# Attention by pairs of graphs, with scores as four row tiles of 32 rows, in a two-layer graph network on one core

## The chip, the cores and the metric

The kernel runs on one core of one Trainium2 chip. A core has five engines that run side by side, each in its own order: TensorE (matrix products), VectorE, ScalarE, GpSimd, and SyncE, which here only issues transfers (DMA). The metric is the device time of one run in microseconds (us). Before the change the median of three runs is 2892.74 us (2891.68 to 2894.03).

## The reference, cut to what matters

Input are 128 graphs of 128 nodes with 256 features each, all in 32-bit floats, and an integer adjacency matrix of 0 and 1 for each graph. Layer 0 has two graph attentions (GAT), a normalisation, a feed-forward of width 1024 and a second normalisation. Layer 1 is attention with 8 heads of 32 features, whose value weights depend on the relation that the adjacency names:

```
q = (src @ Wq + bq);  k = (src @ Wk + bk)              # 8 heads of 32
scores = einsum('bhid,bhjd->bhij', q, k) / sqrt(32)
attn = softmax(scores, axis=-1)
for r in range(4):
    v_r = src @ Wv[r] + bv[r]
    out += einsum('bhij,bhjd->bhid', attn * (adj == r), v_r)
x = layernorm(src + out @ Wo + bo)
x = layernorm(x + gelu(x @ W1 + b1) @ W2 + b2)
```

With an adjacency of 0 and 1 only two relations occur; the program tests this at its start and takes its "binary" arm. Only that arm runs here.

## The kernel before, in words

**Tiling and stages.** Four graphs form a group (G = 4), so there are 32 groups. Each group goes through five stages: load, gat, ff0 (the first feed-forward), att (the attention of layer 1) and ff1. A stage is a Python generator that emits a part of its work and then yields a number of planned time. The function `layers` keeps all stages of all groups in a heap, ordered by planned time: group g starts at PERIOD * g plus the stage's entry in `begin`, and each yield moves it on by an entry of `TIMES`. So stages of several groups are woven into each other. While the plan runs, every TensorE instruction from planned time 280 on, and every transfer from the start, is tied to the one emitted before it. TensorE and the DMA queue of SyncE therefore work in the order of emission, and an instruction that waits holds up all that stand behind it. The other engines get their order from a scheduler when the program is built, and also keep it at run time.

**The attention of a group.** `features` makes the transposed features T of the group's tokens. `transposed` has two ways. The direct one uses TensorE and the identity. The other, taken for all groups but those at the two ends, transposes blocks of 32 by 32 on VectorE (L288), stores the tile with four transfers to a scratch tensor in device memory (L291, `zd`) and loads it back in block order with one transfer (L293). That load must wait until the stores have landed. From T come the queries (L468) and the keys (L474). The keys are written twice by ScalarE (L476) into the tile `kbd`, with a 0/1 factor by row, so that each block of 64 rows holds a block-diagonal matrix of two heads.

`weights(b)` makes the softmax of one graph. Its scores (L490) are four matmuls: for each half i of the features, two row tiles of 64 rows, each with 128 query columns as weights and 256 moving columns of `kbd` (two heads). A 32-bit matmul is two records in the profile, so a graph has 8. Then VectorE takes maxima (L496), ScalarE the exponentials with their sums (L500), VectorE the reciprocals (L501), GpSimd the products (L502); each half of the heads has its own maximum, sum and product. `turned` transposes the weights (tile e to eT) through the same `transposed`. `by_relation` multiplies them with the mask (L515, tile m), `values` makes the values (L531, VectorE adds the bias at L532), `weighted` multiplies weights and values (L544: 16 matmuls of 32 columns by 128, four column tiles side by side, 32 records a graph), and ScalarE copies the result (L548). The product with `wo` (L577) is added to the tokens at L578.

These steps are emitted graph by graph: scores of graphs 0 and 1 first, then for each graph b its weighting, the scores of graph b + 2, the values of b + 1, `wo`, the transpose of b + 2 and the mask of b + 1.

**What runs around it.** `feed_forward` makes ff0 and ff1: products L333 on partial sums (GpSimd, L309 to L312), sums and functions on ScalarE and VectorE (L339 to L360), the second matrix at L378, the addition to the tokens at L388. `gat_block` has its products at L435, L443 and L454, and softmax at L410 to L424; it sends two small rows through device memory (L405, L407). `normalised` takes the statistics on VectorE (L256, L257), some small steps on GpSimd and the scaling on ScalarE (L265); `affine` (L271) is GpSimd's.

PSUM holds eight buffers: seven of the name `mm`, used in turn by all products, and one `av` for L544.

Of the kernel before, what the change touches and what calls it, by code (L numbers as in the profile page):

```python
# [24 lines left out]
P = 128  # L25
G = 4
Q = 32
# [2 lines left out]
TIMES = {  # L30
    "sums": 5, "ff visits": (2.5, 2.5, 3, 3, 3.25, 3.25, 3.25, 3.25), "ff2": 3,
    "ff first half": 10, "ff half": 5, "row": 16, "gat": 19, "wh": 5.5,
    "gat copy": 2, "qk": 4.5, "scores": 5.5, "turn0": 10, "turn1": 5,
    "v0": 5.5, "av": 9, "v": 4, "wo": 4, "turn": 3, "mask": 3,
    "lead ff0": 26, "lead att": 32, "lead ff1": 32, "affine": 7,
    "store": 25,
}
STAGES = "load", "gat", "ff0", "att", "ff1"

GENERAL = dict(  # L40
    binary=False, times=TIMES, period=430, bufs=dict(T=3, tok=2, m=4, mm=6, v=1),
    begin=dict(load=-87, gat=-51, ff0=48, att=132, ff1=300), early={},
    kept={PE: 0, SP: 0},
)

BINARY = dict(
    binary=True, times=TIMES,
    period=100, bufs=dict(T=5, tok=5, m=1, mm=7, v=2),
    begin=dict(load=-87, gat=-51, ff0=48, att=132, ff1=300),
    early={  # L50
        (1, "ff0"): 48,
# [34 lines left out]
def constants(tc, a, c, cst, tmp, ps):  # L86

    nc = tc.nc
    D, DC, R, MW = c.D, c.DC, c.R, c.MW
    T = G * P  # L90
# [55 lines left out]
    def others():  # L146

        ln_rows = cst.tile([P, len(KS), 2, D], F32, name="ln_rows")
        nc.sync.dma_start(ln_rows, on_all_rows(0, 8))
        plus = tmp.tile([P, 3, D], F32, name="plus")  # L150
        nc.sync.dma_start(plus, on_all_rows(8, 3))
        nc.vector.tensor_add(ln_rows[:, :3, 1], ln_rows[:, :3, 1], plus)
        c.ln = {k: (ln_rows[:, n, 0], ln_rows[:, n, 1]) for n, k in enumerate(KS)}
        c.wf2 = wload("wf2")
        c.wq = wload("wq")
        c.wk = wload("wk")
        c.wv = wload("wv")
        c.bv = cst.tile([P, R * D], F32, name="bv")
        nc.sync.dma_start(c.bv, on_all_rows(11, R))
        c.wo = wload("wo")  # L160
        c.w1 = wload("w1")
        c.w2 = wload("w2")
        c.kbd = [cst.tile([P, G, 2, P], F32, name=f"kbd{n}") for n in range(DC)]
        c.own = cst.tile([P, 2], F32, name="own")
        nc.vector.memset(c.own, 0.0)
        for q in range(P // Q):
            nc.vector.memset(c.own[ts(q, Q), q % 2:q % 2 + 1], 1.0)
        c.bk_own = [cst.tile([P, DC], F32, name=f"bk{q}") for q in range(2)]
        c.sums = {n: [cst.tile([P, w.shape[-1] // 2], F32, name=f"{n}s{i}") for i in (1, 2, 4)]
                  for n, w in (("wf1", c.wf1), ("w1", c.w1))}  # L170

# [44 lines left out]
def per_row(v, n):  # L216

    return v[:, :, None].to_broadcast([P, v.shape[-1], n])


def stages_of(tc, a, out, c, pools, plan):
# [73 lines left out]
    def t_tile():  # L295
        return wk.tile([P, G * MW], F32, name="T", bufs=TB)[:, :G * D]
# [162 lines left out]
    def attention(y, g, first, direct):  # L459
# [2 lines left out]
        at = load_mask(g)  # L462
        yield TIMES["lead att"]
        qT = t_tile().rearrange("p (c t) -> p c t", c=DC)
        for i in range(DC):
            p = ps.tile([P, T], F32, name="mm")
            for f in range(DC):
                nc.tensor.matmul(p, c.wq[:, f, ts(i, P)], hT[:, :, f], start=f == 0, stop=f == DC - 1)  # L468
            nc.vector.tensor_scalar(qT[:, i], p, c.col["bq"][:, i:i + 1], SCALE, op0=OP.add, op1=OP.mult)

        for i in range(DC):
            p = ps.tile([P, G, N], F32, name="mm")
            for f in range(DC):
                nc.tensor.matmul(p, c.wk[:, f, ts(i, P)], hT[:, :, f], start=f == 0, stop=f == DC - 1)  # L474
            for q in range(2):
                nc.scalar.activation(c.kbd[i][:, :, q], p, AF.Identity, scale=c.own[:, q:q + 1],  # L476
                                     bias=c.bk_own[q][:, i:i + 1])

        if not binary:
            adj = ps.tile([P, G, N], F32, name="adj", bufs=1)  # L480
            nc.vector.tensor_copy(adj, at)

        def weights(b):


            scores = [ps.tile([P, DC, 2, N], F32, name="mm") for _ in range(2)]
            for i in range(DC):
                for h in range(2):
                    rows = ts(h, P // 2)
                    nc.tensor.matmul(scores[h][:, i], qT[rows, i, ts(b, N)], c.kbd[i][rows, b],  # L490
                                     start=True, stop=True, tile_position=(h * P // 2, 0))
            e = wk.tile([P, H, N], F32, name="e1")
            for h, p in enumerate(scores):
                p = p.rearrange("p c q n -> p (c q) n")
                nm = sm.tile([P, HC], F32, name="nm1")
                nc.vector.tensor_reduce(nm, p, AX.X, OP.max, negate=True)  # L496
                s = sm.tile([P, HC], F32, name="s1")
                eh = e[:, ts(h, HC)]
                for q in range(HC):
                    nc.scalar.activation(eh[:, q], p[:, q], AF.Exp, bias=nm[:, q:q + 1], accum_out=s[:, q:q + 1])  # L500
                nc.vector.reciprocal(s, s)  # L501
                nc.gpsimd.tensor_mul(eh, eh, per_row(s, N))  # L502
            return e

        def turned(e):
            eT = wk.tile([P, H, N], F32, name="eT")
            transposed(e, eT, direct, e)
            return eT
# [27 lines left out]
        def weighted(ms, v):  # L536

            po = ps.tile([P, DC, N], F32, name="av", bufs=1)

            order = range(RV) if binary else range(RV - 1, -1, -1)  # L540
            for i in range(DC):
                for n, r in enumerate(order):
                    for q in reversed(range(HC)):
                        nc.tensor.matmul(po[ts(q, DH), i], v[:, r, i * P + q * DH:i * P + (q + 1) * DH],  # L544
                                         ms[r][:, q // 2 * HC + i * 2 + q % 2],
                                         start=n == 0, stop=n == RV - 1, tile_position=(0, q * DH))
            oT = wk.tile([P, DC, N], F32, name="oT")
            nc.scalar.copy(oT, po)  # L548
            return oT

        RV = 2 if binary else R
        yield TIMES["qk"]
        es = [weights(0)]
        yield TIMES["scores"]
        es.append(weights(1))
        yield TIMES["turn0"]
        eT = [turned(es[0])]
        yield TIMES["turn1"]
        eT.append(turned(es[1]))
        yield TIMES["v0"]  # L560
        PARTS = range(R)
        v, ms = values(0), by_relation(0, eT[0], range(R))
        for b in range(G):
            more = b + 1 < G
            affine(y, "02", b, 1)
            yield TIMES["av"]
            oT = weighted(ms, v)

            if b + 2 < G:
                es.append(weights(b + 2))  # L570
            yield TIMES["v"]
            if more:
                v = values(b + 1)
            yield TIMES["wo"]
            p = ps.tile([P, D], F32, name="mm")
            for i in range(DC):
                nc.tensor.matmul(p, oT[:, i], c.wo[:, i], start=i == 0, stop=i == DC - 1)  # L577
            nc.vector.tensor_add(y[:, b], y[:, b], p)  # L578
            yield TIMES["turn"]
            if b + 2 < G:  # L580
                eT.append(turned(es[b + 2]))
            yield TIMES["mask"]
            if more:
                ms = by_relation(b + 1, eT[b + 1], range(R))
        yield 1
        normalised(y)
        return y
# [11 lines left out]
def layers(ctx: ExitStack, tc: tile.TileContext, a: dict, out: bass.AP, c, plan: dict):  # L599
# [21 lines left out]
    def stage_attention(g):  # L621
        if g == 0:
            folded(nc, c, pools.ps, c.wq, c.col["bq"], "02")
            folded(nc, c, pools.ps, c.wk, c.col["bk"], "02")
            for q in range(2):
                nc.vector.tensor_scalar(c.bk_own[q], c.col["bk"], c.own[:, q:q + 1], None, op0=OP.mult)
# [156 lines left out]
```

## Time and profile before

| what | busy, us | share of 2890.0 us | instructions |
|---|---|---|---|
| TensorE matmuls | 2787.7 | 96% | 15554 |
| TensorE weight loads (beside the matmuls) | 2166.1 | 75% | 15554 |
| ScalarE | 1724.3 | 60% | 5191 |
| GpSimd | 1597.4 | 55% | 1866 |
| VectorE | 1504.7 | 52% | 3072 |
| DMA queue of SyncE, share of 16 engines | | 49.1% | 1156704 packets |

| row of the profile | count | busy, us |
|---|---|---|
| L490, scores, TensorE | 1024 records | 147.7 |
| L544, weighting, TensorE | 4096 records | 211.9 |
| L476, key tile, ScalarE | 128 | 92.6 |
| L500, exponentials, ScalarE | 1024 | 362.1 |
| L502, products, GpSimd | 256 | 269.4 |
| L515, mask, VectorE | 128 | 186.2 |
| idle time of L515 for the transfer eT<-zd | 92 waits | 374.8 |

A row's busy time is the time in which at least one of its instructions is under way; matmuls overlap, so the mean length of one is longer than the distance between two. The chain of waits goes back from the last instruction of the run, at each step to what released it: what stands there set the time. The idle time of an engine that isn't in the chain costs nothing.

### The profile page before, as it was taken

To read this page: it belongs to the slowest core of one execution; us is meant where nothing else is said; L and a number is where in the kernel's file an instruction comes from. 1 tells how busy PE (TensorE), PEld (TensorE's weight loads), DVE (VectorE), ACT (ScalarE), POOL (GpSimd) and SP (SyncE) were. 2 spreads that over 40 slices of the span, in tenths; PEclk is the share of its full clock that TensorE was granted. 3 is DMA by queue.
4 is the path that set the end of the run, shared out by engine and by line. 5 is a ranking of instruction groups with operands and counts; after the bars stand their busy time and mean duration, and the time that the engine had idled before them with its cause. 6 is when DMAs were issued, how large, how long until landed. Compare 5 with 4: busy or idle time off the path is not lost.

```text
span 2890.0 us, 45554 instructions
## 1 busy us (share of the span) xinstructions
PE 2787.7 (96%) x15554; PEld 2166.1 (75%) x15554; DVE 1504.7 (52%) x3072; ACT 1724.3 (60%) x5191; POOL 1597.4 (55%) x1866
## 2 busy tenths in 40 slices
PE   4996999999999999999999999999999999999988
PEld 3764777777877777777777787777778777777756
DVE  5444545545545555554554555555565545555442
ACT  3445566566666666666656666666666675666543
POOL 1434556556655556665655665565566565556553
PEclk7998999999999999999999999999999999999999
DMA  7145454555554556555445545454654544564310
GB/s 275 45 104 121 104 118 106 110 132 127 119 114 107 113 117 139 114 119 118 106 108 131 129 113 125 104 111 117 137 128 107 123 106 111 122 135 106 77 37 15
DMA packets 1156945, 328.69 MB, mean 114 GB/s; under 512 B 903008, under 2 KB 1126752, under 8 KB 1156064
## 3 DMA queue, kind: packets, MB, share of 16 engines
q1 hardware_dynamic: 1156704, 325.68, 49.1%
q8 instruction: 126, 2.06, 0.3%
q14 instruction: 115, 0.94, 0.1%
HBM read 195.97 MB, written 129.62 MB: 113 GB/s over the span
## 4 chain that ended last, share of the span: by engine, by line
PE 71%; DMA 7%; DVE 6%; POOL 5%; ACT 4%; issue 2%; SPq 2%; DVEq 0%; POOLq 0%; ACTq 0%
PE mm L378 25%; PE mm L333 19%; PE mm L531 5%; PE mm L474 4%; PE mm L468 4%; PE mm L490 4%; PE av L544 3%; PE mm L435 3%; PE mm L577 3%; POOL tok L271 2%; DMA zd<-e 2%; SPq L291 2%; DMA eT<-zd 2%; PE mm L454 1%; DMA zd<-T 1%
## 5 line engine op out<-in xcount | busy, mean ns | idle before, releaser
L271 POOL TENSOR_TENSOR tok<-tok,ln_rows 128x512 f32<-128x512 f32 (+1 forms) x596 | 669.5, 1133 | 34.4 <-PE mm L282 11.1
L500 ACT ACTIVATE e<-mm,nm 128x128 f32<-128x128 f32 x1024 | 362.1, 397 | 239.2 <-DVE nm L496 229.6
L378 PE MATMUL mm<-w,fT 128*128 128x256 f32 x2048 | 460.6, 381 | 0.0
L378 PE MATMUL mm<-wf,fT 128*128 128x256 f32 x2048 | 456.6, 381 | 1.5 <-ACT fT L354 1.5
L378 PEld LDWEIGHTS mm<-w,fT 128*128 128x128 f32 x2048 | 386.6, 190 | 74.2 <-issue 24.2
L502 POOL TENSOR_TENSOR e<-e,s 128x512 f32<-128x512 f32 x256 | 269.4, 1053 | 300.5 <-DVE s L501 299.8
L378 PEld LDWEIGHTS mm<-wf,fT 128*128 128x128 f32 x2048 | 386.5, 190 | 64.3 <-issue 9.2
L515 DVE TENSOR_TENSOR m<-eT,am 128x1024 f32<-128x1024 f32 x128 | 186.2, 1454 | 385.2 <-DMA eT<-zd 374.8
L496 DVE TENSOR_REDUCE nm<-mm 128x4 f32<-128x512 f32 x256 | 162.9, 676 | 254.6 <-PE mm L490 254.6
L265 ACT ACTIVATE tok<-tok,nmr,rstd 128x256 f32<-128x256 f32 x480 | 249.9, 603 | 20.1 <-POOL nmr L263 20.0
L531 PE MATMUL mm<-wv,T 128*128 128x512 f32 x512 | 249.3, 610 | 0.0
L352 POOL TENSOR_TENSOR fT<-fT 128x512 f32<-128x512 f32 x128 | 163.3, 1277 | 153.8 <-ACT fT L351 153.8
L500 ACT ACTIVATION_READ_ACCUMULATOR e<-mm,nm 128x1 f32 x1024 | 242.9, 237 | 0.0
L354 ACT ACTIVATE fT<-fT,col 128x512 f32<-128x512 f32 x256 | 170.4, 715 | 118.8 <-DVE fT L348 117.1
L309 POOL TENSOR_TENSOR t<-T 128x256 f32<-128x256 f32 x64 | 47.6, 744 | 321.3 <-DMA T<-zd 321.0
L333 PE MATMUL mm<-T,w 128*128 128x256 f32 x768 | 202.3, 386 | 4.0 <-DMA T<-zd 2.9
L424 POOL TENSOR_TENSOR e<-e,s 128x512 f32<-128x512 f32 (+1 forms) x68 | 68.1, 1002 | 244.4 <-DVE s L423 230.6
L333 PE MATMUL mm<-T,wf 128*128 128x256 f32 x768 | 193.1, 381 | 0.0
L256 DVE BATCH_NORM_STATS2 st<-tok 128x6 f32<-128x256 f32 x480 | 176.7, 409 | 2.4
L333 PEld LDWEIGHTS mm<-T,w 128*128 128x128 f32 x768 | 144.4, 192 | 30.6 <-issue 6.5
L422 ACT ACTIVATE e<-e,nm 128x128 f32<-128x128 f32 x256 | 101.6, 430 | 105.2 <-DVE nm L419 98.8
L333 PEld LDWEIGHTS mm<-T,wf 128*128 128x128 f32 x768 | 146.1, 191 | 21.7 <-issue 0.8
(144 smaller groups left out, 5147.1 us busy)
## 6 DMA issues: line engine op xcount, KB each, us to landing
zd<-e SPq DMA_DIRECT2D x496, 128.0 KB, 4.6
eT<-zd SPq DMA_DIRECT2D x124, 512.0 KB, 4.4
zd<-T SPq DMA_DIRECT2D x364, 128.0 KB, 3.5
T<-zd SPq DMA_DIRECT2D x91, 512.0 KB, 4.2
xt<-in_xT_dram SPq DMA_DIRECT2D x32, 512.0 KB, 5.0
e<-zsd SPq DMA_DIRECT2D x60, 256.0 KB, 3.3
tok<-in_x_dram SPq DMA_DIRECT2D x30, 512.0 KB
out_dram<-tok SPq DMA_DIRECT2D x29, 512.0 KB, 5.4
```

The source lines that it names most:

```text
L256: nc.vector.bn_stats(st, y[:, b])
L265: nc.scalar.activation(y[:, b], y[:, b], AF.Identity, bias=nmr[:, b:b + 1], scale=rstd[:, b:b + 1])
L271: engine.tensor_tensor(y[:, b:b + n], y[:, b:b + n], v[:, None, :].to_broadcast([P, n, D]), op)
L333: nc.tensor.matmul(p[:, i], win[k][:, ts(f0 + i, P)], hs[k], start=first and i == 0, stop=True, skip_group_check=True)
L352: nc.gpsimd.tensor_add(hi[:, :, 1], hi[:, :, 1], hi[:, :, 0])
L354: nc.scalar.activation(lo[:, i], lo[:, i], func, bias=bin_[:, f0 + i:f0 + i + 1])
L378: nc.tensor.matmul(ys[b // 2][:, b % 2], fT[f][:, ts(b, N)], wout[:, f], start=b % 2 == 0 and n == 0, stop=n == FC - 1, skip_group_check=True)
L496: nc.vector.tensor_reduce(nm, p, AX.X, OP.max, negate=True)
L500: nc.scalar.activation(eh[:, q], p[:, q], AF.Exp, bias=nm[:, q:q + 1], accum_out=s[:, q:q + 1])
L502: nc.gpsimd.tensor_mul(eh, eh, per_row(s, N))
L515: nc.vector.tensor_tensor(m, eT, at[:, b][:, None, :].to_broadcast([P, H, N]), OP.mult)
L531: nc.tensor.matmul(p, hT[:, b, f], wv[:, f, r:r + 2], start=f == 0, stop=f == DC - 1)
```

## The change

The attention works on two graphs at a time (`together=2`). The key tile is plain: `kT`, written once by ScalarE. The scores of a pair are 16 matmuls: for each graph and each half of the features, four row tiles of 32 rows (one head each), with 128 query columns as weights and 128 moving key columns. Each of the four row tiles has a PSUM buffer of its own, which holds both graphs and both halves. The purpose is to let four small matmuls run in the array at once and to drop the zeros that the block-diagonal tile carries through it. The softmax then has one maximum for each buffer, one reciprocal for the pair, and one product for each graph. Weights, transposes, masks, values, weighting, `wo` and its addition also go by pairs, so the steps between the yields change, and with them the planned times and the order of emission. Below, "i" is the half of the features and "q" the row tile.

```diff
-    "gat copy": 2, "qk": 4.5, "scores": 5.5, "turn0": 10, "turn1": 5,
-    "v0": 5.5, "av": 9, "v": 4, "wo": 4, "turn": 3, "mask": 3,
+    "gat copy": 2, "qk": 7, "scores": 11, "turn": 14, "mask": 11, "av": 10,
+    "wo": 8, "turned": 3,
...
-    period=100, bufs=dict(T=5, tok=5, m=1, mm=7, v=2),
+    period=100, bufs=dict(T=5, tok=5, m=2, mm=7, v=2),
...
+        kT = wk.tile([P, DC, T], F32, name="kT", bufs=1)
...
-            for q in range(2):
-                nc.scalar.activation(c.kbd[i][:, :, q], p, AF.Identity, scale=c.own[:, q:q + 1],
-                                     bias=c.bk_own[q][:, i:i + 1])
+            nc.scalar.activation(kT[:, i], p, AF.Identity, bias=c.col["bk"][:, i:i + 1])
...
-        def weights(b):
-            scores = [ps.tile([P, DC, 2, N], F32, name="mm") for _ in range(2)]
-            for i in range(DC):
-                for h in range(2):
-                    rows = ts(h, P // 2)
-                    nc.tensor.matmul(scores[h][:, i], qT[rows, i, ts(b, N)], c.kbd[i][rows, b],
-                                     start=True, stop=True, tile_position=(h * P // 2, 0))
-            e = wk.tile([P, H, N], F32, name="e1")
...
+        def weights(bs):
+            n = len(bs)
+            scores = [ps.tile([P, n, DC, N], F32, name="mm") for _ in range(HC)]
+            for j, b in enumerate(bs):
+                for i in range(DC):
+                    for q in range(HC):
+                        rows = ts(q, DH)
+                        nc.tensor.matmul(scores[q][:, j, i], qT[rows, i, ts(b, N)], kT[rows, i, ts(b, N)],
+                                         start=True, stop=True, tile_position=(q * DH, 0))
+            es = [wk.tile([P, DC, HC, N], F32, name="e1") for _ in bs]
+            s = sm.tile([P, HC, n, DC], F32, name="s1", bufs=2)
+            for q, p in enumerate(scores):
+                nm = sm.tile([P, n * DC], F32, name="nm1", bufs=8)
+                nc.vector.tensor_reduce(nm, p.rearrange("p j i n -> p (j i) n"), AX.X, OP.max, negate=True)
+                for j in range(n):
+                    for i in range(DC):
+                        k = j * DC + i
+                        nc.scalar.activation(es[j][:, i, q], p[:, j, i], AF.Exp, bias=nm[:, k:k + 1],
+                                             accum_out=s[:, q, j, i:i + 1])
+            r = sm.tile([P, n, DC, HC], F32, name="r1", bufs=2)
+            nc.vector.reciprocal(r.rearrange("p j i q -> p q j i"), s)
+            for j, e in enumerate(es):
+                es[j] = e.rearrange("p i q n -> p (i q) n")
+                nc.gpsimd.tensor_mul(es[j], es[j], per_row(r[:, j].rearrange("p i q -> p (i q)"), N))
+            return es
...
+        STEP = plan["together"]
         yield TIMES["qk"]
-        es = [weights(0)]
+        es = weights(range(STEP))
         yield TIMES["scores"]
-        es.append(weights(1))
-        yield TIMES["turn0"]
-        eT = [turned(es[0])]
-        yield TIMES["turn1"]
-        eT.append(turned(es[1]))
-        yield TIMES["v0"]
...
+        eT = [turned(e) for e in es]
+        for b in range(0, G, STEP):
+            bs = range(b, b + STEP)
+            yield TIMES["turn"]
+            vs = [values(k) for k in bs]
+            affine(y, "02", b, STEP)
+            yield TIMES["mask"]
+            parts = [(by_relation(k, e, range(R)), v) for k, e, v in zip(bs, eT, vs)]
             yield TIMES["av"]
-            oT = weighted(ms, v)
-
-            if b + 2 < G:
-                es.append(weights(b + 2))
-            yield TIMES["v"]
...
+            oT = weighted(parts)
+            if b + STEP < G:
+                es = weights(range(b + STEP, b + 2 * STEP))
             yield TIMES["wo"]
...
+            if b + STEP < G:
+                yield TIMES["turned"]
+                eT = [turned(e) for e in es]
```

`weighted` takes a pair of graphs with one `av` buffer and one copy, the `wo` products of a pair share a PSUM buffer and one addition, and the tiles `kbd`, `own` and `bk_own` and what fills them are gone. The other arm's plan gets `together=1` and other times; it doesn't run.

More of the change, by code (lines that the diff above doesn't have):

```diff
@@ L40 @@
 GENERAL = dict(
-    binary=False, times=TIMES, period=430, bufs=dict(T=3, tok=2, m=4, mm=6, v=1),
-    begin=dict(load=-87, gat=-51, ff0=48, att=132, ff1=300), early={},
+    binary=False, times=TIMES, together=1, period=560, bufs=dict(T=3, tok=2, m=4, mm=6, v=1),
+    begin=dict(load=-87, gat=-51, ff0=48, att=132, ff1=400), early={},
     kept={PE: 0, SP: 0},
@@ L46 @@
 BINARY = dict(
-    binary=True, times=TIMES,
-    period=100, bufs=dict(T=5, tok=5, m=1, mm=7, v=2),
+    binary=True, times=TIMES, together=2,
+    period=100, bufs=dict(T=5, tok=5, m=2, mm=7, v=2),
     begin=dict(load=-87, gat=-51, ff0=48, att=132, ff1=300),
@@ L162, in others @@
         c.w2 = wload("w2")
[L163 to L168, printed above, removed]
         c.sums = {n: [cst.tile([P, w.shape[-1] // 2], F32, name=f"{n}s{i}") for i in (1, 2, 4)]
@@ L471, in attention @@
         for i in range(DC):
-            p = ps.tile([P, G, N], F32, name="mm")
+            p = ps.tile([P, T], F32, name="mm")
             for f in range(DC):
                 nc.tensor.matmul(p, c.wk[:, f, ts(i, P)], hT[:, :, f], start=f == 0, stop=f == DC - 1)
-            for q in range(2):
-                nc.scalar.activation(c.kbd[i][:, :, q], p, AF.Identity, scale=c.own[:, q:q + 1],
-                                     bias=c.bk_own[q][:, i:i + 1])
+            nc.scalar.activation(kT[:, i], p, AF.Identity, bias=c.col["bk"][:, i:i + 1])
         if not binary:
@@ L481, in attention @@
             nc.vector.tensor_copy(adj, at)
-        def weights(b):
-            scores = [ps.tile([P, DC, 2, N], F32, name="mm") for _ in range(2)]
-            for i in range(DC):
-                for h in range(2):
-                    rows = ts(h, P // 2)
-                    nc.tensor.matmul(scores[h][:, i], qT[rows, i, ts(b, N)], c.kbd[i][rows, b],
-                                     start=True, stop=True, tile_position=(h * P // 2, 0))
-            e = wk.tile([P, H, N], F32, name="e1")
[L493 to L503, printed above, removed]
+        def weights(bs):
[23 more added lines that the diff above has]
+            return es
@@ L534, in values, with weighted @@
             return v
-        def weighted(ms, v):
-            po = ps.tile([P, DC, N], F32, name="av", bufs=1)
+        def weighted(parts):
+            n = len(parts)
+            po = ps.tile([P, n, DC, N], F32, name="av", bufs=1)
             order = range(RV) if binary else range(RV - 1, -1, -1)
[L541 to L547, printed above, removed]
+            for j, (ms, v) in enumerate(parts):
+                for i in range(DC):
+                    for k, r in enumerate(order):
+                        for q in reversed(range(HC)):
+                            nc.tensor.matmul(po[ts(q, DH), j, i], v[:, r, i * P + q * DH:i * P + (q + 1) * DH],
+                                             ms[r][:, i * HC + q],
+                                             start=k == 0, stop=k == RV - 1, tile_position=(0, q * DH))
+            oT = wk.tile([P, n, DC, N], F32, name="oT", bufs=1)
             nc.scalar.copy(oT, po)
@@ L551, in attention @@
         RV = 2 if binary else R
+        STEP = plan["together"]
         yield TIMES["qk"]
-        es = [weights(0)]
+        es = weights(range(STEP))
         yield TIMES["scores"]
-        es.append(weights(1))
-        yield TIMES["turn0"]
-        eT = [turned(es[0])]
-        yield TIMES["turn1"]
-        eT.append(turned(es[1]))
-        yield TIMES["v0"]
[L561 to L565, printed above, removed]
-            yield TIMES["av"]
-            oT = weighted(ms, v)
-            if b + 2 < G:
-                es.append(weights(b + 2))
-            yield TIMES["v"]
-            if more:
-                v = values(b + 1)
-            yield TIMES["wo"]
[L575 to L584, printed above, removed]
+        eT = [turned(e) for e in es]
[6 more added lines that the diff above has]
+            parts = [(by_relation(k, e, range(R)), v) for k, e, v in zip(bs, eT, vs)]
+            yield TIMES["av"]
+            oT = weighted(parts)
+            if b + STEP < G:
+                es = weights(range(b + STEP, b + 2 * STEP))
+            yield TIMES["wo"]
+            p = ps.tile([P, STEP, D], F32, name="mm")
+            for j in range(STEP):
+                for i in range(DC):
+                    nc.tensor.matmul(p[:, j], oT[:, j, i], c.wo[:, i], start=i == 0, stop=i == DC - 1)
+            nc.vector.tensor_add(y[:, b:b + STEP], y[:, b:b + STEP], p)
+            if b + STEP < G:
+                yield TIMES["turned"]
+                eT = [turned(e) for e in es]
         yield 1
@@ L624, in stage_attention @@
             folded(nc, c, pools.ps, c.wk, c.col["bk"], "02")
-            for q in range(2):
-                nc.vector.tensor_scalar(c.bk_own[q], c.col["bk"], c.own[:, q:q + 1], None, op0=OP.mult)
             folded(nc, c, pools.ps, c.wv, c.bv, "02", rows=True)
```

## The prediction

> **What bounds the kernel now.** I read the page's shares first, then the chain of waits over one group in mid run, then the DMA queue's timeline, then the few places where TensorE stood still. The page:
>
> ```profile
> PE 2787.7 (96%) x15554; PEld 2166.1 (75%) x15554; DVE 1504.7 (52%) x3072; ACT 1724.3 (60%) x5191; POOL 1597.4 (55%) x1866
> PE 71%; DMA 7%; DVE 6%; POOL 5%; ACT 4%; issue 2%; SPq 2%; DVEq 0%; POOLq 0%; ACTq 0%
> ```
>
> TensorE is near full, nothing else above 60%. The chain of waits from 1400 to 1500 us (start, length, what):
>
> ```profile
> 1410.69 1.06 PE mm L490 x8
> 1411.75 1.01 PE av L544 x32
> 1412.76 1.06 PE mm L490 x8
> 1413.83 3.65 PE mm L378 x16
> ...
> 1481.96 3.43 PE mm L468 x8
> 1485.40 3.43 PE mm L474 x8
> 1488.83 6.91 PE mm L378 x32
> 1495.74 1.06 PE mm L490 x8
> ```
>
> Every piece is TensorE's and each begins where the last ends: from the first scores of one group to those of the next, 85.05 us (85.2 over 27 groups) without a wait. So shorter TensorE work shows at once, and so does any new wait of TensorE. The transposes run beside it, on one DMA queue, and in order:
>
> ```profile
> 1424.64 2.56 SPq L291 DMA_DIRECT2D zd<-e  x4
> 1430.01 0.38 SPq L293 DMA_DIRECT2D eT<-zd  x1
> 1430.49 4.21 SPq L291 DMA_DIRECT2D zd<-e  x4
> 1437.31 0.38 SPq L293 DMA_DIRECT2D eT<-zd  x1
> ...
> 1480.49 4.64 SPq L291 DMA_DIRECT2D zd<-T  x4
> 1487.78 0.38 SPq L293 DMA_DIRECT2D T<-zd  x1
> ```
>
> One transpose is four stores and a load that the queue issues only when the stores have landed; the queue can't begin the next before that. From the first store to the load's issue it takes 4.9 to 5.4 us when the queue was idle before, 6.9 to 7.1 right behind another transpose (means over 22 or 23 groups), and the load lands 4.2 to 4.4 us later. Last, the start of the run, where TensorE did wait:
>
> ```profile
> 242.19 0.66 PE L544 MATMUL av<-eT,v 128*32 128x128 f32 x8 [11.96 <-DMA eT<-zd]
> ...
> 246.88 2.73 PE L531 MATMUL mm<-wv,T 128*128 128x512 f32 x4
> 229.00:256.00 27.00, 11.13 (x92) 6.41 (x92) 10.41 (x18) 11.15 (x50) 9.21 (x12) 0.73 0.61 126
> ```
>
> After the wait the four value products take 2.73 us instead of 1.72, at a mean granted clock of 0.73 (from 300 to 2600 us: 1.00).
>
> **What the Trainium skill says.** "TensorE: Matmul & The Clock Gate", Part 3: matmuls on different row groups run at the same time; four row tiles of 32 rows were measured 3.07 times as fast at 512 columns. The trace agrees for two tiles: the starts of a pair of L490 lie 7 ns apart and the pairs 215 ns, what one full 256-column record takes. Same page, LDWEIGHTS: a load's time goes by columns, not rows, about 107 ns for 128. In the trace one-column matmuls on full weights (L192) follow each other at 112 ns, and the two loads of a L490 pair start 7 ns apart, so row tiles load in parallel. Same page, HAM oscillation: an idle gap beyond some 3.4 us brings the clock back to half. Here idle gaps of 3.1 to 4.4 us were followed by 3.4 to 6.8 us at half clock. "DMA: Bandwidth & Descriptors", Rules for kernel authors: a DMA that reads what another wrote must wait for its completion before it is issued; that is the queue's wait above (L293 on zd<-e, 327 us in 245 waits).
>
> **The change, part by part.** Scores: a graph has 4 matmuls, 8 records in 4 pairs: 4 x 0.215 + 0.2 for the change of array shape = 1.06 us, 4.26 for a group. After: per pair of graphs 32 records in 8 fours. A four of 128-column matmuls on 32-column tiles (L544) takes 0.109 us in the trace, and full 128-column transposes with 128-column weight loads (L282) follow at 0.109 too. I take 0.109, since loads are parallel; if the four took turns at loading it would be 0.43. A block is 8 x 0.109 + 0.2 = 1.07 us, two make 2.14: 2.1 us less per group. L544 by pairs: 2 x (16 x 0.109 + 0.14) = 3.77 instead of 4 x 1.01: 0.27 less. Three excursions from full shape instead of four, at 0.1 us on either side: 0.2 less. Sum 2.6: **82.6 us of TensorE work in a group**.
>
> On other engines nothing decides: ScalarE has two key writes instead of four of 0.77 us; GpSimd four products of 1024 columns (1.70 us by the slope from 0.71 at 256 to 1.04 at 512) instead of eight of 1.05; VectorE as many maxima, fewer reciprocals. All lie beside TensorE. The scores take four of seven PSUM buffers at once, but four exponentials at 0.34 us free one each, and the fourth later user comes 7 us on.
>
> The order of work is what costs. As built, the changed program has behind the second scores block (graphs 2 and 3) on TensorE: L372 x8 (3.45 us), wo x4 (1.72), L448 x4 (1.73), L327 x8 (3.45), values x4 (3.44), L327 x14 (6.04), L429 x4 (1.75), L327 x2 (0.86), L429 x4 (1.75), L327 x4 (1.72), their weighting (1.88), then the queries of the next group: 28.0 us with the edges. The DMA queue has for the same stretch: both weight transposes of the pair, and only then the transpose of the next group's features T, which those queries read. Before, this T stood between the weights of graphs 2 and 3 and landed some 5 us ahead of L468. The chain now, from the end of the second scores:
>
> - VectorE is 1.0 late (the second GAT weighting's maxima and a 0.68 addition stand ahead); first maximum 0.9: 1.9.
> - 16 exponentials at 0.34 (before, 8 per graph), as the one reciprocal waits for all: 7.4; reciprocal 7.6; product of the first graph 9.3.
> - VectorE has 3.1 us of GAT sums ahead of the transpose (1.24): 11.9.
> - Queue: first weights, load issued 5.2 later; second 0.45 + 6.9; T 0.45 + 7.05; landing 4.3: **36.3 us**.
>
> TensorE would be there at 28.0, so the queries wait 8.3 us. Part of it shows sooner: the second graph's load lands near 28.8 and its mask product ends near 30.3, where its weighting wants it at 27.1. Behind the queries everything of TensorE is held up, as it issues in order. The idle pieces are long enough for the half clock; gaps of 3.1 to 4.4 us in this trace cost 1.7 to 2.7 us each, so I add 2.0.
>
> From the queries to the end of the second scores I sum 54.3 us from the same rows; the first pair's chain there (about 30 us) is hidden under 34.7 us of TensorE work. Period: 54.3 + 36.3 + 2.0 = **92.6 us instead of 85.2**, 7.4 more. It applies to groups 2 to 30 (group 31 transposes on TensorE, the first ones run before the order is fixed): 29 x 7.4 = 215; the other three save 2.6 each. 2893 + 215 - 8 = **3100 us**.
>
> Bounds: least, VectorE free at once and the queue at its fastest (10.0 + 4.9 + 6.3 + 6.3 + 0.9 + 4.3 = 32.7) and no clock loss: 87.0, +1.8 a group, 2937. Most, 39.5 us (queue at 7.3 to 8.0 each) and 3.4 of clock: 97.2, 3233.
>
> **Rivals.**
> - No wait: the chain hides, TensorE's 2.6 us come out whole, 32 x 2.6 = 83, **2810**. For it speaks that TensorE waits for nothing now; against it that even the least chain (32.7) is longer than 28.0, and faster than before needs one under 30.7.
> - Only the weighting waits, T being early enough: 3.2 us less clock and overlap, 82.6 + 2.7 + 1.0 = 86.3, +1.1 a group: **2917**. Against it: one queue, in order, with T third.
> - Row tiles load one after the other: blocks of 3.6 us, 5.0 more a group on top of my case: **3245**. Against it: the 7 ns between the loads of a pair.
>
> **How the numbers follow.** My case 0.84, no wait 0.07, weighting only 0.05, serial loads 0.04. The time is that of my case. Its bounds, less their corners, give 2940 to 3190. Faster 0.08, same 0.03, slower 0.89.
>
> **What would show it.** In the profile after: the scores' row x8 fours at about 1.07 us a block; TensorE's share under 92%; the chain of waits running through DMA and its queue each group; the queries waiting for DMA T<-zd by 4 to 8 us, the weighting for m or eT by 1 to 3; granted clock under 0.95. I am wrong if the queries wait for nothing, if T lands less than 31 us after the second scores' end, or if the scores' block is far from 1.07.

## The result and the profile after

The change makes the kernel slower: a median of 3200.58 us in four runs (3196.29 to 3202.96), beside 2893.03 for the kernel before (four runs, three of them those named at the top). The ratio is 1.106, with a 95% interval of 1.104 to 1.108. The forecast was slower by 207 us, to 3100; it is slower by 307, and the time lies 11 us above the top of the forecast's range of 2940 to 3190.

The page of the kernel after: the shares of the engines, the granted clock in 40 slices, the shares of the chain of waits, and the row of the queries.

```profile
PE 2812.0 (88%) x16578; PEld 2172.2 (68%) x16578; DVE 1505.3 (47%) x2809; ACT 1675.4 (52%) x5063; POOL 1553.0 (49%) x1610
PEclk6996999999999999999999999999999999999989
PE 48%; DMA 13%; POOL 9%; ACT 8%; issue 8%; SPq 7%; DVE 6%; POOLq 0%; DVEq 0%; ACTq 0%
L463 PE MATMUL mm<-T,wq 128*128 128x512 f32 x256 | 172.2, 835 | 150.6 <-DMA T<-zd 150.6
```

TensorE falls from 96% to 88% of a longer span, and no other engine rises. TensorE's part of the chain falls from 71% to 48%, and 20% now lie on transfers and their queue (DMA and SPq). The last line names the place: the queries (L463, L468 before) stand idle for 150.6 us, all of it for the transposed features T.

The chain of waits of the kernel after over one group (start, length, what). Lines left out are short pieces, and one of VectorE by which the profile joins TensorE to the queue:

```profile
1417.78 1.10 PE mm L484 x32
1418.89 3.65 PE mm L372 x16
...
1439.18 3.42 DMA zd<-e
...
1442.68 0.38 SPq L287
...
1447.06 3.04 DMA zd<-T
...
1450.23 4.54 DMA T<-zd
1454.78 0.14 issue
1454.91 5.50 PE mm L463 x8
1460.41 3.43 PE mm L468 x8
```

Before, every piece of this stretch was TensorE's. Now the time from the second scores (L484, end at 1418.88) to the queries (1454.91) goes through the stores and loads of the transposes. The same pieces one group later, where they stand further apart than on the mean, on the DMA queue of the kernel after (the second scores end at 1512.57 there, the queries begin at 1549.60):

```profile
1524.60 2.67 SPq L285 DMA_DIRECT2D zd<-e  x4
1530.03 0.38 SPq L287 DMA_DIRECT2D eT<-zd  x1
1530.51 4.45 SPq L285 DMA_DIRECT2D zd<-e  x4
1537.52 0.38 SPq L287 DMA_DIRECT2D eT<-zd  x1
1537.94 4.57 SPq L285 DMA_DIRECT2D zd<-T  x4
1545.15 0.38 SPq L287 DMA_DIRECT2D T<-zd  x1
```

Three transposes stand in one row: 5.4, 7.0 and 7.2 us from first store to load issue, and then 4.45 us until the queries begin. T was ready for its stores at 1528.05, where VectorE's transpose of that tile ended; they began 9.9 us later, because the queue is in order. TensorE's timeline of that stretch, with the idle time ahead of a group of instructions in brackets, and its window (busy times of TensorE, its weight loads, VectorE, ScalarE and GpSimd, then the granted clock, the DMA share and GB/s):

```profile
1542.13 0.43 PE L544 MATMUL av<-eT,v 128*32 128x128 f32 x8 [2.33 <-DMA eT<-zd]
1543.39 0.43 PE L544 MATMUL av<-m,v 128*32 128x128 f32 x8 [0.84 <-DVE m L513]
...
1549.60 5.94 PE L463 MATMUL mm<-T,wq 128*128 128x512 f32 x8 [5.16 <-DMA T<-zd]
1555.38 3.60 PE L468 MATMUL mm<-T,wk 128*128 128x512 f32 x8
```

```profile
1538.00:1556.00 18.00, 9.68 (x78) 4.83 (x77) 2.62 (x4) 3.98 (x10) 1.17 (x1) 0.72 0.72 152
```

Three gaps of 2.3, 0.8 and 5.2 us make 8.3, and then the queries take 5.94 us where the keys, of the same size, take 3.60: for 10.2 us of this window the clock was at half (0.72 on the mean). Over 27 groups the gaps are smaller: 5.1 us ahead of the queries and 1.2 in the weighting. TensorE's list of waits for the whole run (us in total, times, longest) has two kinds, those for transfers and a kind that the forecast did not have:

```profile
PE mm L463 <- DMA T<-zd: 150.6, 30, 6.7
PE av L544 <- DMA eT<-zd: 35.1, 18, 11.9
PE mm L327 <- ACT fT L333: 31.2, 28, 1.1
PE av L544 <- DVE m L513: 19.5, 24, 1.4
PE mm L327 <- ACT fT L340: 18.5, 24, 2.0
```

The feed-forward's products (L327) wait for ScalarE's copies once or twice in each group. The place between the first and the second scores, on TensorE and then on ScalarE of the kernel after:

```profile
1578.24 1.03 PE L327 MATMUL mm<-t,wf1s 128*128 128x256 f32 x4
1580.38 1.10 PE L327 MATMUL mm<-t,wf1s 128*128 128x256 f32 x4 [1.11 <-ACT fT L333]
...
1587.00 1.13 PE L327 MATMUL mm<-T,wf 128*128 128x256 f32 x4 [0.34 <-ACT fT L340]
```

```profile
1570.60 0.37 ACT L494 ACTIVATE e<-mm,nm 128x128 f32<-128x128 f32 x1 [7.53 <-DVE nm L490]
...
1575.75 0.45 ACT L494 ACTIVATE e<-mm,nm 128x128 f32<-128x128 f32 x1
...
1576.09 2.15 ACT L259 ACTIVATE tok<-tok,nmr,rstd 128x256 f32<-128x256 f32 x4
...
1579.60 0.64 ACT L333 COPY fT<-mm 128x512 f32<-128x512 f32 x1
```

All 16 exponentials of the first pair stand in one row, 5.6 us, with the scaling of the tokens and four exponentials of GAT behind them. The copy that TensorE waits for from 1579.27 begins only at 1579.60, right behind them.

### The profile page after: what moved, and what is told of

The parts are those of the page before. It is cut to its first block, busy times and chain, and to the rows that moved or that the text cites. A ratio compares the mean times of both kernels' runs of the same rounds, so it can differ in the third digit from the quotient of the medians.

```text
span 3194.1 us, 46824 instructions
## 1 busy us (share of the span) xinstructions
PE 2812.0 (88%) x16578; PEld 2172.2 (68%) x16578; DVE 1505.3 (47%) x2809; ACT 1675.4 (52%) x5063; POOL 1553.0 (49%) x1610
## 4 chain that ended last, share of the span: by engine, by line
PE 48%; DMA 13%; POOL 9%; ACT 8%; issue 8%; SPq 7%; DVE 6%; POOLq 0%; DVEq 0%; ACTq 0%
PE mm L372 16%; PE mm L327 10%; SPq L285 6%; PE mm L463 5%; PE mm L529 4%; DMA T<-zd 4%; ACT e L494 4%; DMA zd<-T 3%; POOL tok L265 3%; PE mm L468 3%; DMA zd<-e 3%; PE mm L572 3%; POOL e L500 2%; ACT tok L259 2%; DVE st L250 2%
## 5 line engine op out<-in xcount | busy, mean ns | idle before, releaser
L265 POOL TENSOR_TENSOR tok<-tok,ln_rows 128x512 f32<-128x512 f32 x476 | 647.2, 1378 | 40.8 <-PE mm L276 14.5
L372 PE MATMUL mm<-w,fT 128*128 128x256 f32 x2048 | 460.8, 381 | 0.0
L372 PE MATMUL mm<-wf,fT 128*128 128x256 f32 x2048 | 456.8, 381 | 2.3 <-ACT fT L348 1.3
L372 PEld LDWEIGHTS mm<-w,fT 128*128 128x128 f32 x2048 | 386.6, 190 | 67.9 <-issue 14.5
L372 PEld LDWEIGHTS mm<-wf,fT 128*128 128x128 f32 x2048 | 387.1, 190 | 58.7 <-ACT fT L348 1.7
L500 POOL TENSOR_TENSOR e<-e,r 128x1024 f32<-128x1024 f32 x128 | 240.0, 1896 | 219.5 <-DVE r L497 219.5
L463 PE MATMUL mm<-T,wq 128*128 128x512 f32 x256 | 172.2, 835 | 150.6 <-DMA T<-zd 150.6
L529 PE MATMUL mm<-wv,T 128*128 128x512 f32 x512 | 238.7, 605 | 19.0 <-ACT wh L438 13.2
L469 ACT ACTIVATE kT<-mm,col 128x512 f32<-128x512 f32 x64 | 43.9, 686 | 373.3 <-PE mm L468 373.3
L463 PEld LDWEIGHTS mm<-T,wq 128*128 128x128 f32 x256 | 67.0, 275 | 237.3 <-issue 237.2
L253 POOL TENSOR_SCALAR rstd<-mv 128x4 f32<-128x4 f32 x129 | 30.9, 240 | 381.5 <-DVE mv L251 375.2
L327 PE MATMUL mm<-T,w 128*128 128x256 f32 x768 | 200.8, 385 | 13.4 <-ACT fT L340 13.2
L464 DVE TENSOR_SCALAR T<-mm,col 128x512 f32<-128x512 f32 x64 | 48.0, 750 | 325.0 <-PE mm L463 325.0
L573 DVE TENSOR_TENSOR tok<-tok,mm 128x512 f32<-128x512 f32 x60 | 40.9, 681 | 339.7 <-PE mm L572 338.9
```

What stands on the lines that cost most here:

```text
L327: nc.tensor.matmul(p[:, i], win[k][:, ts(f0 + i, P)], hs[k], start=first and i == 0, stop=True, skip_group_check=True)
L372: nc.tensor.matmul(ys[b // 2][:, b % 2], fT[f][:, ts(b, N)], wout[:, f], start=b % 2 == 0 and n == 0, stop=n == FC - 1, skip_group_check=True)
L500: nc.gpsimd.tensor_mul(es[j], es[j], per_row(r[:, j].rearrange("p i q -> p (i q)"), N))
L529: nc.tensor.matmul(p, hT[:, b, f], wv[:, f, r:r + 2], start=f == 0, stop=f == DC - 1)
```

## The experiments

"Period" is the mean time from one group's queries to the next's, over 27 groups in mid run. It is 85.23 us before and 94.70 after. Ratios are to the kernel before on the same chip, with a 95% interval. "Row tiles" stands for the four tiles of 32 rows with the plain key tile. Single groups scatter by 1 to 2 us about the mean in most of these kernels, so differences of a few tenths in the period are uncertain.

| kernel | us | ratio | period |
|---|---|---|---|
| e2, pairs with the old scores | 3198.55 | 1.1053 (1.1035 to 1.1072) | 95.69 |
| e3, T on TensorE | 3082.58 | 1.0650 (1.0628 to 1.0672) | 91.15 |
| e7, T between the weights | 3310.49 | 1.1451 (1.1432 to 1.1470) | 99.08 |
| e6, clock kept | 3167.09 | 1.0959 (1.0940 to 1.0977) | 94.10 |
| e4, more room | 2945.41 | 1.0186 (1.0166 to 1.0205) | 86.98 |
| e8, e4 with half the exponentials | 2888.38 | 0.9998 (0.9989 to 1.0007) | 85.43 |
| e11, after with half the exponentials | 3098.31 | 1.0714 (1.0698 to 1.0729) | 91.80 |
| e10, e4 with GAT earlier | 3116.31 | 1.0786 (1.0770 to 1.0801) | 92.55 |
| e1, row tiles alone | 2917.90 | 1.0109 (1.0068 to 1.0150) | 86.01 |
| e5, e1 with a first block for two graphs | 2910.63 | 1.0072 (1.0055 to 1.0089) | 86.18 |
| e9, e1 with the second block later | 2906.84 | 1.0062 (1.0049 to 1.0075) | 85.78 |
| e12, row tiles for graphs 2 and 3 | 2879.92 | 0.9957 (0.9943 to 0.9971) | 84.86 |

### Which half of the change costs: e2

The kernel after, with the scores of before: two tiles of 64 rows and the block-diagonal keys, in the new order by pairs.

```diff
...
-                    for q in range(HC):
-                        rows = ts(q, DH)
-                        nc.tensor.matmul(scores[q][:, j, i], qT[rows, i, ts(b, N)], kT[rows, i, ts(b, N)],
+                    for h in range(2):
+                        rows = ts(h, P // 2)
+                        nc.tensor.matmul(scores[j][h][:, i], qT[rows, i, ts(b, N)], c.kbd[i][rows, b],
...
```

> The order of work by pairs of the changed kernel, with the old two row tiles of 64 rows and the block-diagonal key tile. My theory: all the waits of the changed kernel stay, and each of the two scores blocks of a group is 1.0 us longer and lies on the path from the queries to the second scores: 3200 + 29 x 2.1 = about 3260 us. Rival (the row tiles are what is slow): back towards 2893 us.

It takes as long as the kernel after, and the queries wait as they do there:

```profile
PE mm L468 <- DMA T<-zd: 165.5, 30, 6.9
```

From second scores to queries it is 36.23 us, and 36.26 in the kernel after. The work by pairs in its order is the loss, and the row tiles neither cause it nor relieve it. The scores' block of a pair takes 1.93 us against 1.10, yet from queries to second scores the two differ by 1.0 us only (59.46 and 58.44), not by the 1.66 of two blocks: between first and second scores TensorE waits 0.9 us a group for ScalarE here and 1.7 in the kernel after, so the rest comes back there. The forecast that this kernel would be 60 us slower than the one after missed.

### Where the transfer of T stands: e3 and e7

e3 takes T off the queue: TensorE transposes it directly ahead of the queries.

```diff
-        hT = features(y, first or direct)
         at = load_mask(g)
-        yield TIMES["lead att"]
...
+            yield TIMES["lead att"]
+            hT = features(y, True)
```

> The changed kernel with the features T of the attention transposed by TensorE just ahead of the queries, so the DMA queue has two transposes and not three between the second scores and the queries. My theory (three transposes in a row on one queue set the time): the wait of the queries for DMA goes, the wait of the weighting for the second graph's mask stays (to about 30 us after the scores), then 8 transposes and their copies, some 2.5 us: a group takes about 90 instead of 95 us, 3050 us. Rival (16 exponentials and one reciprocal for the pair, ahead of any transpose, set it): hardly under 3180.

The wait for T is gone, and so are 119 us (1.1062 less 1.0650, of 2893), although TensorE now has the transposes to do; 150 had been expected. What is left: the weighting's waits for weights stay, and the queries wait a little for their copies.

```profile
PE av L548 <- DMA eT<-zd: 57.1, 32, 11.9
...
PE mm L467 <- DVE T L278: 25.4, 29, 0.9
```

e7 puts T's transpose between those of the two graphs, as it stood before the change. The added yield is taken off the next one, so the rest keeps its planned times.

```diff
...
-                eT = [turned(e) for e in es]
+                eT = [turned(es[0])]
+                yield TIMES["turned b"]
+                eT += [turned(e) for e in es[1:]]
```

> The changed kernel with the features T put on the DMA queue between the two weight transposes of the second pair, as they stood in the kernel before; nothing else is moved on TensorE. My theory (three transposes on one queue don't fit into 28 us): the queries no longer wait for T, but the second graph's weighting waits in its place until about 38 us after the scores, 3190 to 3240 us. Rival (it is T's place, third, that costs): the second weights' wait is hidden, 2950 us or less.

The queries wait for nothing now, and the weighting pays instead, with more than was expected. Its line in the list of waits, then the queue:

```profile
PE av L544 <- DMA eT<-zd: 285.3, 33, 12.1
```

```profile
1481.90 0.38 SPq L287 DMA_DIRECT2D eT<-zd  x1
...
1485.33 2.51 SPq L285 DMA_DIRECT2D zd<-T  x4
```

T wasn't ready when its turn came, so the queue stood for 3 us, and the second weights behind it came later still: from second scores to queries it takes 4.0 us more than in the kernel after. At these planned times, moving T within the row only moves the wait. T ahead of both wasn't run with them.

### Whether the distance is the whole of it: e4

e4 changes the planned times alone, so that more of TensorE's work stands between the pair's scores and what reads the transposes. This also moves T ahead of the second pair's weights on the queue, so the distance and the order of the queue change together.

```diff
-    "gat copy": 2, "qk": 7, "scores": 11, "turn": 14, "mask": 11, "av": 10,
+    "gat copy": 2, "qk": 7, "scores": 13, "turn": 14, "mask": 11, "av": 20,
```

> The changed kernel with other planned times alone (the yield ahead of the weighting 20 for 10, the one after the scores 13 for 11), so that the weighting of a pair stands some 50 us of TensorE work behind its scores and not 26, and T stands ahead of the weights on the queue. My theory: the waits for DMA go, what is left is TensorE's 82.6 us a group and up to 2.2 us of waits for ScalarE: 2815 to 2880 us. Rival (the pair itself costs, by its bursts on the other engines): above 3000.

253 of the 307 us go (8.76% of 2893), with no instruction changed. In the 27 groups TensorE waits for no transfer any more. The ends recover too: of the 51.2 us by which its profiled span is still longer, 27 x 1.748 = 47.2 lie in the periods, so 4.0 lie outside them, where the kernel after has 48.3. But it isn't faster than before either, and my 2815 to 2880 missed:

```profile
PE mm L327 <- ACT e L494: 33.9, 28, 1.8
PE mm L327 <- issue: 25.0, 41, 1.8
...
PE mm L327 <- ACT fT L333: 12.5, 25, 1.0
```

What is left are waits of the feed-forward's products: 2.4 us a group behind the second scores, half of it for the exponentials and most of the rest for ScalarE's copies, and 0.6 behind the first. For those that the list puts to "issue" the profile names no releaser.

### What the half clock costs: e6

Twelve products without use fill the gap ahead of the queries.

```diff
+        if binary and not (first or direct):
+            p = ps.tile([P, 2, D], F32, name="mm")
+            for _ in range(12):
+                nc.tensor.matmul(p[:, 0], c.wo[:, 0, :P], c.wo[:, 1], start=True, stop=True)
```

> The changed kernel with 12 matmuls of 256 columns, 5.2 us, of which nothing is used, between the weighting of the second pair and the queries, where TensorE stands idle for 5 to 6 us. If the half clock costs what I charged (2.0 us a group), the queries start where they did and run at full clock, 3.4 us instead of 5.4: 3200 - 29 x 1.9 = 3145 us. If the clock isn't on the path: 3200 us, or more by what of the 5.2 us doesn't fit the gap.

TensorE's timeline and window there:

```profile
1435.08 5.45 PE L463 MATMUL mm<-wo 128*128 128x256 f32 x24
1440.56 3.70 PE L467 MATMUL mm<-T,wq 128*128 128x512 f32 x8
```

```profile
1433.00:1451.00 18.00, 17.11 (x89) 11.43 (x90) 2.95 (x4) 1.96 (x3) 2.69 (x4) 1.00 0.63 138
```

The queries now run at full clock: 3.5 us a group instead of 5.35. Between 300 and 2600 us the time at half clock falls from 181 us to 48. But the period falls by 0.60 only, between my two cases. Of the 1.9 us saved, 0.9 are lost from second scores to queries: these stand right behind the filling products (1435.08 + 5.45), and on the mean begin some 0.9 us after T has landed, where it was 0.1. The other 0.4 are longer waits between first and second scores, most of them for ScalarE's copies of GAT. So the queries' half clock costs 1.9 us a group, as charged, but this run shows only 0.6 of it in the period, in part because its own filling is too long for the gap.

### What ScalarE's burst costs: e8, e11 and e10

e8 (from e4) and e11 (from the kernel after) make one exponential of 256 columns out of two of 128, so that a pair has 8 instead of 16. They leave out the maxima and sums of the second half, so their times show only what the burst costs.

```diff
-                    for i in range(DC):
-                        k = j * DC + i
-                        nc.scalar.activation(es[j][:, i, q], p[:, j, i], AF.Exp, bias=nm[:, k:k + 1],
-                                             accum_out=s[:, q, j, i:i + 1])
+                    nc.scalar.activation(es[j][:, :, q], p[:, j], AF.Exp, bias=nm[:, j * DC:j * DC + 1],
+                                         accum_out=s[:, q, j, 0:1])
+            nc.vector.tensor_copy(s[:, :, :, 1], s[:, :, :, 0])
```

> e4 with half the exponentials: one instruction of 256 columns for both halves of the features, with the first half's maximum and one sum for both, which leaves out the maxima and sums of the second half. A pair's burst on ScalarE falls from 16 x 0.34 = 5.5 to some 8 x 0.5 = 4 us and the buffers are free sooner. If the waits of the feed-forward's products left in e4 (about 4.4 us a group) are for this burst, they shrink by a third to a half: 2945 - 29 x 2 = about 2890 us. If they are for the number of buffers that the scores take at once, whatever the burst: 2930 us or more.

> The changed kernel with half the exponentials (as in e8; the maxima and sums of the second half are left out). What I left out of my sum was 2.2 us a group between the first scores and the second, where the feed-forward's products wait for ScalarE's copies behind the 16 exponentials. If the burst is the cause, this stretch falls from 40.9 to about 39.3 us, and the chain behind the second scores from 36.3 to 34.8 by the shorter burst: 3.1 us a group, 3110 us. If the products wait for something else, the stretch stays at 40.9 and only the chain shortens: 3155 us.

e8 takes 1.55 us off the period of e4 and lands on the time of before. e11 takes 2.90 off that of the kernel after: 1.72 in the chain from second scores to queries (34.54), where the exponentials stand ahead of the transposes, and 1.17 from first to second scores (39.76 instead of 40.93), where they stand ahead of the copies. The queries stay at 5.35 us, half clock. So the burst is shown, in both places. Of e11's list, the first two rows; the row for L333, 31.2 us in the kernel after, is gone:

```profile
PE mm L463 <- DMA T<-zd: 130.5, 30, 6.4
PE mm L327 <- ACT fT L345: 31.1, 29, 3.2
```

The waits for L345 grew from 13.4 us, but in the 27 groups all of them lie behind the second scores, in the stretch whose length T's transfer sets. In e8 one wait is left, 1.6 us a group, behind the first scores. TensorE, then what ScalarE does at that place:

```profile
1420.39 1.10 PE L327 MATMUL mm<-t,wf1s 128*128 128x256 f32 x4 [2.88 <-issue]
```

```profile
1416.69 1.28 ACT L404 ACTIVATE e<-e,wh 128x128 f32<-128x128 f32 x4 [10.97 <-DMA e<-zsd]
```

ScalarE had stood 11 us for the small row that GAT sends through device memory, and its exponentials follow behind that. That this row causes the wait is likely, but not shown. e10 meant to test that by planning GAT earlier in e4.

```diff
-    begin=dict(load=-87, gat=-51, ff0=48, att=132, ff1=300),
+    begin=dict(load=-87, gat=-64, ff0=48, att=132, ff1=300),
```

> e4 with the GAT stage 13 planned units earlier, so that its small row goes through the DMA queue ahead of a feature transpose. In e4 ScalarE stands 8.6 us for this row just ahead of the pair's exponentials, and with it the PSUM buffers of the scores. If this wait is what is left over TensorE's 82.6 us, beside the burst (e8), the 4.4 us of waits in e4 fall to about 2: 2945 - 29 x 2.4 = 2875 us. If the burst alone holds the buffers: 2935 us or more.

It tells nothing of the question. GAT's products now wait for their input, and the scores for their keys, and these two waits hide what it was made for:

```profile
PE mm L429 <- DMA xt<-in_xT_dram: 107.6, 29, 5.9
PE mm L484 <- ACT kT L469: 73.7, 29, 3.7
```

How much of the remaining loss is that row's stays open; at that place, behind the first scores, TensorE waits 0.6 us a group in e4 and 1.6 in e8.

### What the row tiles bring by themselves: e1, e5, e9 and e12

e1 is the kernel before, graph by graph, with row tiles and the plain key tile.

```diff
-            scores = [ps.tile([P, DC, 2, N], F32, name="mm") for _ in range(2)]
+            scores = [ps.tile([P, DC, N], F32, name="mm") for _ in range(HC)]
...
-                    nc.tensor.matmul(scores[h][:, i], qT[rows, i, ts(b, N)], c.kbd[i][rows, b],
-                                     start=True, stop=True, tile_position=(h * P // 2, 0))
+                    nc.tensor.matmul(scores[q][:, i], qT[rows, i, ts(b, N)], kT[rows, i, ts(b, N)],
+                                     start=True, stop=True, tile_position=(q * DH, 0))
```

> The four row tiles and the plain key tile in the order of the kernel before, graph by graph. My theory (the order of work by pairs costs, the row tiles gain): a scores block of one graph takes 4 x 0.109 + 0.2 = 0.64 us instead of 1.06, nothing new is waited for, 4 x 0.42 x 32 = 54 us less: about 2838 us. Rival (row tiles of 32 rows, with twice as many weight loads, are what is slow): above 2893 us, blocks longer than 1.06 us.

My theory that they bring some 54 us by themselves fell. (e1, e5 and e9 also take four maxima of 256 columns a graph in place of two of 512; what that costs wasn't taken apart.) TensorE's timeline of e1, the blocks of graphs 0 and 1:

```profile
1420.03 0.73 PE L482 MATMUL mm<-kT,T 32*128 32x128 f32 x16
...
1421.69 0.88 PE L482 MATMUL mm<-kT,T 32*128 32x128 f32 x4
1422.79 0.48 PE L482 MATMUL mm<-kT,T 32*128 32x128 f32 x2 [0.21 <-ACT e L492]
```

A block alone takes 0.66 us to the start of what follows, instead of 1.06, as worked out. But two blocks want eight PSUM buffers and seven exist, so the second waits for the exponentials of the first and takes 2.43 us. e5 gives graphs 0 and 1 one block of four buffers:

```diff
-        es = [weights(0)]
+        es = weights([0, 1])
         yield TIMES["scores"]
-        es.append(weights(1))
```

> As e1, but the scores of graphs 0 and 1, which stood 1 us apart and of which the second waited 1.8 us for a PSUM buffer, are one block in four buffers; graphs 2 and 3 and all that follows stay graph by graph. My theory (the row tiles gain on TensorE, and in e1 the fifth to eighth buffer asked for at once took the gain back): 86.0 us a group less 1.8 and less 0.2 for one block fewer: 84.0, 2840 to 2855 us. Rival (a pair's 16 exponentials in one burst cost what they save): 2890 us or more.

No scores wait for a buffer, the block takes 1.10 us, and the period stays (86.18). The waits have moved to the feed-forward, for ScalarE:

```profile
PE mm L327 <- ACT fT L345: 39.2, 25, 2.0
...
PE mm L372 <- ACT fT L354: 7.7, 21, 0.4
```

e9 keeps e1's two blocks and plans the second one later.

```diff
-    "gat copy": 2, "qk": 4.5, "scores": 5.5, "turn0": 10, "turn1": 5,
+    "gat copy": 2, "qk": 4.5, "scores": 9.5, "turn0": 6, "turn1": 5,
```

> e1 with the scores of graph 1 four planned units later (the yield behind the first scores 9.5 for 5.5, the next one 6 for 10), so that 3.5 us of TensorE work stand between the two blocks and the first four PSUM buffers are free again. My theory: the 1.8 us of waiting in e1 go, 86.0 becomes 84.2 us a group, about 2860 us, faster than both kernels. Rival (what TensorE saves is lost to the order of the other engines, as in e5): 2900 us or more, with new waits of the feed-forward's products for ScalarE.

Again the buffer's wait goes, and again waits of L327 and L372 for ScalarE come. e12, last, uses row tiles only for graphs 2 and 3, whose blocks stand alone between other work, and leaves graphs 0 and 1 as they were (`by_rows` holds e1's scores and softmax):

```diff
             if b + 2 < G:
-                es.append(weights(b + 2))
+                es.append(by_rows(b + 2))
...
```

> The kernel before with the row tiles of 32 rows for graphs 2 and 3 alone, whose scores stand far apart; graphs 0 and 1 keep the block-diagonal tile of 64 rows, so nowhere are more than four PSUM buffers asked for at once. My theory: 2 x 0.4 us of TensorE work less a group and no new wait, 2893 - 27 = about 2866 us, faster than both kernels. Rival (what TensorE saves comes back as waits for ScalarE in the feed-forward, as in e5 and e9): 2885 us or more.

It takes 2879.92 us, less than both kernels, though the gain of 0.4% is only half of what was expected: of 0.8 us saved on TensorE in a group, 0.37 reach the mean period. The periods one by one tell more: most often a period is 84.31 us here and 85.05 before, so 0.74 come out there. Single longer groups take the rest, above all the first of the 27: its queries take 8.18 us instead of 3.43, with a wait of 3.0 us for VectorE in them, and its period is 89.06.

## Why the prediction fell short, step by step

- **"A block is 8 x 0.109 + 0.2 = 1.07 us."** Right: 1.10. The fours follow each other at 0.112 us, the first two at 0.214, and within a four the starts lie 7 ns apart. The rival with loads in turn is out. Where the block of L544 doesn't wait, it takes 1.88 us, as summed.
- **"T 0.45 + 7.05; landing 4.3: 36.3 us."** The mechanism is right, and the sum too: 36.26 over 27 groups. That it fits so well is in part luck: the first store begins 11.1 us after the second scores instead of 11.9, and the queue with the landing takes 25.2 instead of 24.4, so two errors of 0.8 cancel. The place of the waits was right: 5.1 us ahead of the queries and 1.2 in the weighting, for 4 to 8 and 1 to 3. e3, e4 and e7 show that the row of transfers makes these waits; the first rival (no wait) and the second (weighting only) did not come about.
- **"I add 2.0" for the clock.** Right: the queries take 5.35 us instead of 3.43, 1.92 more. The gaps of "3.1 to 4.4 us" it rests on are counted from the start of the record before; the brackets of the trace show 2.7 to 3.8 for them.
- **"On other engines nothing decides", and "four exponentials at 0.34 us free one each, and the fourth later user comes 7 us on".** This step failed; it put the burst of exponentials at nothing. I counted the scores' own PSUM buffers, but not that ScalarE, in order, serves nobody else while it works off 16 exponentials. From queries to second scores I had 56.3 us with the clock; it took 58.44. Up to the first scores the trace agrees (17.51), and behind them it took 40.93, some 2.1 more than the sum leaves. TensorE waits there 1.7 us a group for ScalarE, 1.1 of it for the copies behind the burst. In e11, 1.17 us go with half the exponentials. Of the rest, some 0.6 are waits for GAT's copies that e11 still has; what makes them wasn't tested. The period is 9.47 us longer instead of 7.4: 56 us over 27 groups.
- **"29 x 7.4 = 215; the other three save 2.6 each."** The ends failed as well. From the start to the queries of group 2 it took 24.94 us more than before, over the last two periods 14.70, and from the last queries to the end 8.63: 48.3, where two periods' gain of 7.4 less 8 had been put, 7. That is the other 41 us. At the start the trace shows longer waits (3.14 us of the scores for kT, 4.72 for weights) and half clock for most of 250 to 284 us. I had taken groups outside the fixed order as free of the new row, and they are not: e4, which changes the planned times alone, has 4.0 us there. How the 44 us divide among these waits wasn't tested.

The sum: 24.94 + 27 x 9.474 + 14.70 + 8.63 = 304.1 us, the difference of the two profiled spans (3194.1 and 2890.0). So the mechanism and its largest terms were right. Two terms, the waits for ScalarE in each period and the ends, were put at nothing or at a gain; together they make the 97 us by which the change was undersized in this profile (56 + 41).

## What to carry to other kernels

Where a product passes through a queue that works in order, count two lengths from the same event: the microseconds of the bounding engine's work between producer and reader, and the chain with all that stands ahead in the queue. Grouping changes both, since it puts requests in a row and takes away work between them; here some 28 us stood against 36. And when the bounding engine gets faster or its inputs come in larger lots, look at the engine next to it for bursts: here what TensorE saved on the scores came back as waits for ScalarE and for PSUM buffers, except where the blocks stood alone (e12).

## What the runs showed of the hardware

- Four row tiles of 32 rows with 128-column loads and 128 moving columns run every 112 ns in 32-bit floats, about as long as one full 128-column record (109 ns): four for one, loads included. In these kernels they ask for four PSUM buffers at once.
- In the group shown, gaps of 2.3, 0.8 and 5.2 us within 10 us came with 10.2 us of half clock; over 27 groups the stretches last 3.4 to 13.7 us, and the eight matmuls of the queries take 1.9 us more. "TensorE: Matmul & The Clock Gate" of the Trainium skill, HAM oscillation, speaks of idle gaps over some 3.4 us. The traces agree only in part: in the group shown the half clock begins 0.5 us ahead of the gap of 5.2 us, and in e6 each of the 13 stretches of half clock between 300 and 2600 us (3.4 to 6.8 us long) comes with gaps of 2.4 us at most. Filling products kept the clock where they ran (1.00 in the window above, 0.72 without).
- A transpose of 512 KB through device memory takes 5.4 us from first store to the load's issue when the queue was idle and 7.0 to 7.3 right behind another one (means of the kernel after), though the tiles are of equal size. Why it takes longer there wasn't tested.
